# Attention scores of a tile in three rows, and up to two tiles between scores and the sum over values

## The chip, the cores and the metric

One core of a Trainium2 chip runs the whole program in one launch. The metric is the device time of that launch in microseconds (us), as the median of several runs. All data and all matmuls are float32.

## What is computed

The input `x` has 4 batches of 384 channels on a 32 x 32 grid (1024 positions). Two layers follow each other.

Layer 0 adds to `x` a two-dimensional selective scan of its group norm. Each batch is scanned in four directions; per direction and channel 16 states follow `h = h * exp(dt * A) + dt * u * B`, and the output is the sum of `h * C` over the states. The four directions are added, normalised over the channels and put through GELU.

Layer 1 treats the positions as tokens `t` of 384 numbers:

```python
t = t + attention(layernorm(t))    # 6 heads of 64; a token sees itself and the 64 before it
t = t + experts(layernorm(t))      # 4 experts 384 -> 1536 -> 384, the best 2 of each token, weighted
```

In the reference the attention of a head is `softmax(mask(q k^T / 8)) v`, and the heads' outputs are multiplied by a gate and a 384 x 384 matrix.

## The kernel before, in words

**Scan.** A batch makes 192 scan steps, 768 in all. A step covers 32 channels x 4 states of one direction over the 1024 positions, as a `[128, 1024]` tile: ScalarE makes the decay `exp(dt * a)` (`decay`, into one of two PSUM tiles `dA`), GpSimd multiplies by B (`times_b`), VectorE scans (`scan`), GpSimd or VectorE multiplies by C (`times_c`), and TensorE sums the states (`fold_y`, into a bank `ps_y`). `time_steps` prepares `dt`.

**Tokens.** When the scan of a batch is complete, `tokens(b)` (line 967) takes its 1024 tokens as 8 tiles of 128, `TILES = 3` of them in flight at once (line 1202). A tile goes through `tile(a)`: load (`yl`, `tt`), norm, GELU, norm, transposes, the queries `q` and keys `k`, the last 64 keys of the tile before (line 1048, after that tile is in `scored`), the values `v`. Then it waits at line 1065 until fewer than `CORES` tiles are in the list `core`. Inside the core it makes the scores (`score`, line 1071: for a pair of head pairs and one head of each pair, matmuls into a bank `ps_s`, then a masked copy with row maximum by VectorE), gives back `q` (line 1093), takes the exponentials on ScalarE in place (line 1099), turns them by transposes (`turn`, line 1106: one head pair into a bank `ps_p`, copied to `pt`, of which there are 3), takes a row for the result `o` (line 1125), sums over the values into a bank `ps_o`, scales (line 1143) and leaves the core (line 1148). The output matrix, a norm and the router's logits follow.

**Experts.** `route(n)` takes half a batch (4 tiles), ranks the experts of its tokens and scatters the tokens to slots in DRAM sorted by expert (`scatter`, row `tks`). A batch makes 19 expert tiles of 128 slots, 76 in all: `hidden` runs 72 matmuls into banks `ps_hid`, `output` 24 matmuls into a bank `y_ff`. `combine(b)` (line 1464) gathers each token's two results, adds them to the residual and writes the output; before the last batch it takes four rows at once (line 1474) for one tile.

**Shared stocks.** A `Stock` (line 78) is a set of buffers that a generator waits for. What matters here: `rows`, `NROW = 10` buffers of `[128, 384]`, shared by tokens (`yl`, `tt`, `xt`, `q`, `v`, `o`, `ot`, `xlt`), routing (`tks`) and combining (`cb`); `srows`, 4 buffers of `[128, 384]` for the scores of one tile; `pts_`, 3; `keys`, 2; `banks`, 4 PSUM banks for everything but `dA`. A waiter for one buffer is served in order of its rank (0 for the scan's banks, 1, and `HID_RANK = 2` for `ps_hid`); a waiter for several is served when so many are free. When the last scan is done, the scan's large buffers join `rows` and its two PSUM tiles join `banks` (lines 879 to 886).

**Order of the work.** Nothing is ordered by hand. While the program is built, `Machine` (line 218) runs all these generators against a model of the five engines with estimated durations, and emits each instruction when the model would start it. Among those that could start, the one with the lowest ready time plus bias goes first: `EARLY = -6` us for tokens and routing, 0 for the scan, `LATER = +6` us for the expert tiles and for combining. On the chip each engine then runs its queue in that fixed order. A change of a stock or of a limit can so move any later instruction of the program.

**Constants.** `b2_sb`, the experts' output bias, is a `[4, 384]` tile loaded at line 421 and used at line 1502 with the router's weights `gt` (line 1480). `gt_sb`, a `[32, 384]` tile of ones and zeros (lines 446 to 455), is used by the group norm.

Of the kernel before, what the change touches and what calls it, by code (L numbers as in the profile page):

```python
# [11 lines left out]
F32 = mybir.dt.float32  # L12
# [5 lines left out]
P = 128  # L18
B, D, HH, WW = 4, 384, 32, 32
L = HH * WW  # L20
T = D // P
# [4 lines left out]
GROUPS = 32  # L26
# [7 lines left out]
KW = WIN + P  # L34
NE, HID = 4, 4 * D
# [14 lines left out]
GELU_BIAS = EARLY  # L50
FAVOUR = 1.0
TILES, EPS, NZ = 3, 1e-5, 7
CORES = 1
NEG = -1.0e30


# [336 lines left out]
def conv_attn_hybrid(  # L393
# [7 lines left out]
    nc = tc.nc  # L401
    const = ctx.enter_context(tc.tile_pool(name="const", bufs=1))
    dram = ctx.enter_context(tc.tile_pool(name="dram", bufs=2, space=bass.MemoryType.DRAM))

    def const_load(src, shape, name):
        dst = const.tile(shape, F32, name=name)
        nc.sync.dma_start(dst, src)
        return dst
# [9 lines left out]
    vb_sb = const_load(vb.rearrange("(t p) -> p t", p=P), [P, T], "vb_sb")  # L418
    gw_sb = const_load(gw, [P, T, NE], "gw_sb")
    gb_sb = const_load(gb.partition_broadcast(P), [P, NE], "gb_sb")  # L420
    b2_sb = const_load(b2, [NE, D], "b2_sb")

    ident = const.tile([P, P], F32, name="ident")
    make_identity(nc, ident)
# [15 lines left out]
        base=0, channel_multiplier=1,  # L440
# [2 lines left out]
        gm, gm, pattern=[[-P, T], [GC, GROUPS]], compare_op=ALU.is_ge, fill=0.0,  # L443
        base=GC - 1, channel_multiplier=-1,
    )
    gt_sb = const.tile([GROUPS, D], F32, name="gt_sb")
    nc.gpsimd.memset(gt_sb, 1.0)
    nc.gpsimd.affine_select(
        gt_sb, gt_sb, pattern=[[1, D]], compare_op=ALU.is_ge, fill=0.0,
        base=0, channel_multiplier=-GC,  # L450
    )
    nc.gpsimd.affine_select(
        gt_sb, gt_sb, pattern=[[-1, D]], compare_op=ALU.is_ge, fill=0.0,
        base=GC - 1, channel_multiplier=GC,
    )

    mask = const.tile([P, KW], F32, name="mask")
# [3 lines left out]
        base=0, channel_multiplier=1,  # L461
# [3 lines left out]
        base=WIN, channel_multiplier=-1,  # L465
# [3 lines left out]
        base=0, channel_multiplier=-1,  # L469
# [7 lines left out]
        base=0, channel_multiplier=-1,  # L477
# [6 lines left out]
    m = Machine(nc)  # L484
# [7 lines left out]
    with tc.tile_pool(name="setup", bufs=1) as setup:  # L492
# [12 lines left out]
            base=0, channel_multiplier=1,  # L505
# [3 lines left out]
        for j in range(JB):  # L509
            ps = banks.now("ps_al")  # L510
# [17 lines left out]
    work = ctx.enter_context(tc.tile_pool(name="work", bufs=1))  # L528
# [5 lines left out]
    xbs, xbts, hss, ybs = (  # L534
        Stock(m, work, tag, n, [P, D]) for tag, n in (("xb", 1), ("xbt", 2), ("hs", NHS), ("yb", 1))
    )
    srows = Stock(m, work, "sr", 4 * CORES, [P, D])
    us_all = Stock(m, work, "u", 2, [P, L])
    eds = Stock(m, work, "ed", 3, [P, HB])
    keys = Stock(m, work, "key", 2, [P, T * KW])  # L540
# [40 lines left out]
    def copy(dst, src):  # L581

        if on_vector():
            yield from dve.tensor_copy(dst, src)
        else:
            yield from act.copy(dst, src)

    def on_vector():
        lead = FAVOUR if count_of["scan"] < NSLOT else 0.1
        return m.clock["dve"] + lead < m.clock["act"]  # L590
# [376 lines left out]
    def tokens(b):  # L967
# [18 lines left out]
        def tile(a):  # L986
# [11 lines left out]
            ps = yield from three("ps_y0", w)  # L998
            yield from normal_of(w, ps)
            g = yield from three("ps_g", w)  # L1000
            mm = Calls()
# [8 lines left out]
            ps = yield from three("ps_t", tt)  # L1010
            yield from normal_of(w, ps)
            xt = yield from rows.take("xt")
            ps = yield from three("ps_x1", w)
# [7 lines left out]
            for n, (w, dst) in enumerate(  # L1021
                ((wq, q[:, :D].rearrange("p (t l) -> p t l", t=T)), (wk, kv[:, :, :P]))
            ):
                ps = yield from banks.take("ps_qk")
                mm = Calls()
# [26 lines left out]
            ps = yield from banks.take("ps_v")  # L1052
            mm = Calls()
# [10 lines left out]
            n_keys = KW if a else P  # L1064
            yield lambda: len(core) < CORES
            core.append(a)
            mx = rp.tile([P, 2, HEADS], F32, tag="mx", name="mx")
            sums = rp.tile([P, HEADS], F32, tag="sums", name="sums")
            s = yield from srows.take("s", n=4)

            def score(hps, j):
                ps = yield from banks.take("ps_s")
                r = slice(j * HD, (j + 1) * HD)
                mm = Calls()
                for n, hp in enumerate(hps):
                    mm.matmul(
                        ps[:, n * KW : n * KW + n_keys],
                        q[r, ts(hp, P)], k[r, hp * KW : hp * KW + n_keys],
                        start=True, stop=True,
                    )  # L1080
                yield from pe.all(mm)
                for n, hp in enumerate(hps):
                    h = 2 * hp + j
                    c = slice(n * KW, n * KW + n_keys)
                    yield from dve.tensor_tensor_reduce(
                        s[hps[0] + j][:, c], ps[:, c], mask[:, :n_keys], 1.0, NEG,
                        ALU.add, ALU.max, mx[:, 0, h : h + 1],
                    )
                banks.give(ps)
# [5 lines left out]
            for hp in range(T):  # L1095
                for j in range(2):
                    h = 2 * hp + j
                    sj = s[hp // 2 * 2 + j][:, hp % 2 * KW : hp % 2 * KW + n_keys]
                    yield from act.activation(
                        sj, sj, AF.Exp, bias=mx[:, 1, h : h + 1], scale=scale,  # L1100
                        accum_out=sums[:, h : h + 1],
                    )
# [1 line left out]
            pts = {}  # L1104

            def turn(hp):
                base, c0 = hp // 2 * 2, (hp % 2) * KW
                pt = yield from pts_.take("pt")
                ps = yield from banks.take("ps_p")
                mm = Calls()  # L1110
                for j in range(2):
                    mm.transpose(ps[:, ts(j, P)], s[base + j][:, c0 : c0 + P], ident)
                for j in range(2 if a else 0):
                    mm.transpose(ps[:, ts(2 + j, P)], s[base + j][:, c0 + KW - P : c0 + KW], ident)
                yield from pe.all(mm)
                if hp > 0:
                    srows.give(s[base], s[base + 1])
                yield from copy(pt[:, : 2 * P], ps[:, : 2 * P])
                if a:
                    yield from copy(pt[WIN:, 2 * P :], ps[WIN:, 2 * P : 4 * P])  # L1120
                banks.give(ps)
                pts[hp] = pt
# [4 lines left out]
            mm = Calls()  # L1127
# [22 lines left out]
            ps = yield from three("ps_ot", o)  # L1150
# [3 lines left out]
            ps = yield from banks.take("ps_pr")  # L1154
            on_act = not on_vector()
            mm = Calls()
# [10 lines left out]
            for o in range(T):  # L1167
                c = ts(o, P)
# [12 lines left out]
            ps = yield from three("ps_t2", tt)  # L1181
# [6 lines left out]
            ps = yield from three("ps_xt", tt)  # L1188
            rows.give(tt)
            yield from copy(xt[:, :D], ps[:, :D])  # L1190
            mm = Calls()
# [272 lines left out]
    def combine(b):  # L1464

        def one(a):
            n, a_in = 2 * b + a // PT, a % PT
            if b == B - 1:
                yield lambda: n in routed
            xs, idx, p, eid, gate = routed[n]  # L1470
            if b == B - 1:
                o, gt = yield from rows.take("cb", n=2)
            else:
                o, gt, *gs = yield from rows.take("cb", n=4)
            yield from sp.dma_start(
                o[:, :D].rearrange("p (t l) -> p t l", t=T), t2dr[b][:, :, ts(a, P)]
            )
            ps = yield from banks.take("ps_gt")
            yield from pe.transpose(ps[:NE, :P], p[:, a_in, :], ident)
            yield from copy(gt[:NE, :P], ps[:NE, :P])  # L1480
            banks.give(ps)
            if b == B - 1:
                yield lambda: ("experts", b) in have
                gs = yield from rows.take("cb", n=2)
            for n in range(2):
                yield from pool.indirect_dma_start(
                    out=gs[n][:, :D], out_offset=None, in_=ysdr[b % 2],
                    in_offset=bass.IndirectOffsetOnAxis(ap=idx[:, n, a_in : a_in + 1], axis=0),
                )
            yield m.settled(*gs)  # L1490
            ps = yield from banks.take("ps_c")
            yield from act.activation(ps[:, :D], gs[0][:, :D], AF.Copy, scale=gate[:, 0, a_in : a_in + 1])
            yield from dve.scalar_tensor_tensor(
                gs[0][:, :D], gs[1][:, :D], gate[:, 1, a_in : a_in + 1], ps[:, :D], ALU.mult, ALU.add
            )
            mm = Calls()
            for t in range(T):
                c = ts(t, P)
                mm.matmul(ps[:, c], gs[0][:, c], ident, start=t == 0, stop=False)
            for t in range(T):  # L1500
                c = ts(t, P)
                mm.matmul(ps[:, c], b2_sb[:, c], gt[:NE, :P], start=False, stop=t == T - 1)
            yield from pe.all(mm)
            rows.give(gt, *gs)
            yield from dve.tensor_tensor(o[:, :D], ps[:, :D], o[:, :D], ALU.add)
            banks.give(ps)
            yield from sp.dma_start(
                out[b].rearrange("(t p) h w -> p t (h w)", p=P)[:, :, ts(a, P)],
                o[:, :D].rearrange("p (t l) -> p t l", t=T),
            )  # L1510
            rows.give(o)

        yield from m.together([one(a) for a in range(NT)], 2 if b < B - 1 else NT, LATER)
        have.add(("out", b))

# [82 lines left out]
```

## Time and profile before

| | |
|---|---|
| median of 3 runs | 3890.63 us (3870.85 to 3907.89) |
| the profiled execution | 3882.5 us, its span 3880.8 us |
| TensorE matmul, busy | 3033.4 us (78%), 15868 matmuls |
| VectorE, busy | 2940.7 us (76%) |
| GpSimd, busy | 2824.4 us (73%) |
| ScalarE, busy | 2226.8 us (57%) |
| mean granted TensorE clock | 0.822 of full speed |
| DMA | 953.65 MB, 246 GB/s |
| last scan step starts | 3201.9 us |

Read it as two stretches. Until 3202 us the scan runs, with the tokens and experts of finished batches beside it; after that there is no scan, and what is left are the remaining expert tiles, the tokens of the last batch and their experts. The shares in the table are averages over both.

The timeline gives the stages of the tokens, from the first transposes of the first tile to those before the last tile's logits: 782 to 1154 us for batch 0, 1617 to 2194 for batch 1, 2461 to 2904 for batch 2 and 3236 to 3499 for batch 3. Expert tiles leave (`yb`) from 1100 to 1613 us for batch 0, 2074 to 2868 for batch 1, 2907 to 3495 for batch 2 and 3510 to 3835 for batch 3.

### The profile page before, as it was taken

What the parts mean: (1) busy time and instruction counts of PE and PEld (TensorE: products, weight loads), DVE (VectorE), ACT (ScalarE), POOL (GpSimd) and SP (SyncE); (2) the same over time, 40 slices, a digit from 0 to 9 for tenths busy, and PEclk for the clock granted to TensorE, in tenths of its full rate; (3) what the DMA queues carried; (4) which work ended last, traced back from release to release, by engine and by line L of the source; (5) the groups of instructions that cost most, each with busy time, mean ns of one, the idle gap of its engine ahead of it and who ended that gap; (6) DMA issues with size and microseconds to landing.
All of it is one profiled execution on the core that took longest, in us unless ns stands there. A gap on an engine that the chain in (4) does not pass through costs nothing. (4 is left out here: it accounts for less than half of the span.)

```text
span 3880.8 us, 50273 instructions
## 1 busy us (share of the span) xinstructions
PE 3033.4 (78%) x15868; PEld 1841.7 (47%) x15868; DVE 2940.7 (76%) x3358; ACT 2226.8 (57%) x4017; POOL 2824.4 (73%) x1474
## 2 busy tenths in 40 slices
PE   2555555577697988777768889899787899998997
PEld 1100010045464555344345545566555557876886
DVE  2999999998888998888888899988788992332001
ACT  2545454467586777755557767778675763432221
POOL 1999989988898877888888699889787981012001
PEclk6555556678798999876678989899898999998997
DMA  5775775544478998734357989776568975459995
GB/s 202 266 273 204 270 268 203 174 143 149 171 253 333 341 374 324 285 127 164 112 208 254 329 301 347 270 254 213 203 228 295 388 272 184 136 167 327 318 318 182
DMA packets 394145, 953.65 MB, mean 246 GB/s; under 512 B 49620, under 2 KB 173400, under 8 KB 393880
## 3 DMA queue, kind: packets, MB, share of 16 engines
q1 hardware_dynamic: 385688, 925.27, 68.1%
q0 software_dynamic: 8192, 25.17, 1.9%
q8 instruction: 126, 2.06, 0.2%
q14 instruction: 139, 1.14, 0.1%
HBM read 786.39 MB, written 182.78 MB: 250 GB/s over the span
## 5 line engine op out<-in xcount | busy, mean ns | idle before, releaser
L148 POOL TENSOR_TENSOR z<-dts,bc 128x1024 f32<-128x1024 f32 x768 | 1792.9, 2359 | 186.7 <-PE ps_y L159 105.8
L148 ACT ACTIVATE dA<-dts,a 128x1024 f32<-128x1024 f32 x768 | 854.6, 1118 | 536.8 <-DVE z L148 512.1
L159 PE MATMUL ps_y<-z,fold 128*32 128x512 f32 x3072 | 725.8, 765 | 436.2 <-POOL z L148 237.2
L148 DVE TENSOR_TENSOR_SCAN dA<-dA,z 128x1024 f32<-128x1024 f32 x409 | 935.6, 2288 | 93.2 <-ACT dA L148 77.7
L148 POOL TENSOR_TENSOR z<-z,bc 128x1024 f32<-128x1024 f32 x359 | 841.7, 2355 | 110.8 <-DVE z L148 96.2
L148 DVE TENSOR_TENSOR_SCAN z<-dA,z 128x1024 f32<-128x1024 f32 x359 | 807.8, 2276 | 31.6 <-ACT dA L148 28.6
L159 PEld LDWEIGHTS ps_hid<-xbt,w_sb 128*128 128x128 f32 x5472 | 667.0, 198 | 137.2 <-issue 38.3
L159 PE MATMUL y_ff<-w_sb,hs 128*128 128x384 f32 x1824 | 680.8, 515 | 58.5 <-ACT hs L159 46.4
L159 PE MATMUL ps_hid<-xbt,w_sb 128*128 128x128 f32 x5472 | 692.0, 284 | 33.1 <-ACT hs L148 8.2
L148 DVE TENSOR_TENSOR z<-dA,bc 128x1024 f32<-128x1024 f32 x409 | 499.1, 1220 | 13.8 <-DVE dA L148 0.5
L159 PEld LDWEIGHTS ps_y<-z,fold 128*32 128x32 f32 x3072 | 93.1, 120 | 872.8 <-POOL z L148 412.8
L148 ACT ACTIVATE hs<-ps_hid,bb 128x128 f32<-128x128 f32 x912 | 274.1, 365 | 391.8 <-PE ps_hid L159 320.2
L159 PEld LDWEIGHTS y_ff<-w_sb,hs 128*128 128x128 f32 x1824 | 341.3, 199 | 314.9 <-issue 65.9
L148 POOL DMA_INDIRECT cb<-ysdr,idx x64 | 62.6, 979 | 293.7 <-DMA ysdr<-yb 269.8
L159 POOL TENSOR_TENSOR rn<-rn,half 128x1 f32<-128x1 f32 x96 | 52.7, 549 | 266.7 <-DVE rn L159 209.0
L148 DVE COPY yb<-y_ff 128x384 f32<-128x384 f32 x22 | 12.2, 556 | 251.5 <-PE y_ff L159 204.9
L148 POOL DMA_INDIRECT xsdr<-tks,idx x64 | 65.2, 1018 | 146.5 <-DVE idx L159 58.4
L148 ACT ACTIVATE ed<-ps_dt,dtb_sb 128x512 f32<-128x512 f32 x192 | 125.8, 681 | 67.6 <-PE ps_dt L148 59.8
L148 PE MATMUL ps_dt<-xd,dtw_sb 12*128 12x512 f32 x192 | 136.7, 822 | 24.7 <-DMA dtw_sb<-in_dtw_dram 14.2
L148 DVE TENSOR_TENSOR ps_dt<-ps_dt,ed 128x512 f32<-128x512 f32 x192 | 132.6, 690 | 12.3 <-ACT ps_dt L148 9.5
L148 ACT COPY ed<-ps_dt 128x512 f32<-128x512 f32 x96 | 56.0, 584 | 124.8 <-DVE ed L148 124.5
L304 ACT ACT_TABLE_LOAD x80 | 102.6, 1283 | 2.2 <-PEq L1583 0.8
(204 smaller groups left out, 3411.2 us busy)
## 6 DMA issues: line engine op xcount, KB each, us to landing
w_sb<-wl SPq DMA_DIRECT2D x608, 576.0 KB
dts<-dtr SPq DMA_DIRECT2D x384, 512.0 KB
bc<-xdr SPq DMA_DIRECT2D x128, 512.0 KB
dtr<-ed SPq DMA_DIRECT2D x192, 256.0 KB
ub<-udr SPq DMA_DIRECT2D x48, 512.0 KB
yp<-ydr SPq DMA_DIRECT2D x96, 256.0 KB
ydr<-yp SPq DMA_DIRECT2D x96, 256.0 KB
wl<-in_w_dram SPq DMA_DIRECT2D x32, 576.0 KB
```

The source lines that it names most:

```text
L148: return getattr(self.real, op)(*a, **k)
L159: getattr(self.real, op)(*a, **k)
L304: self.nc.scalar.add_instruction(mybir.InstLoadActFuncSet(name=self.nc.get_next_instruction_name(), act_func_set_id=EXP_LN_SET,))
```

## The change

- `CORES` goes from 1 to 2: two tiles may be between the start of their scores and the scaling of their result.
- The scores of a tile lie in three rows of `[128, 384]` in place of four: one row for each pair of heads, its two heads side by side. `srows` has 3 x 2 = 6 buffers in place of 4.
- `turn` gives a row back as soon as its own head pair is turned. Before, two rows held the heads of two pairs and were given back after the second of these.
- `b2_sb` and `gt_sb` become two parts of one tile of 36 partitions; the bias lies on partitions 32 to 35, and so the router's weights that are multiplied with it are copied to partitions 32 to 35 of `gt`.

```diff
-CORES = 1
+CORES = 2
...
-    b2_sb = const_load(b2, [NE, D], "b2_sb")
+    group_rows = const.tile([GROUPS + NE, D], F32, name="group_rows")
+    gt_sb, b2_sb = group_rows[:GROUPS], group_rows[GROUPS:]
+    nc.sync.dma_start(b2_sb, b2)
...
-    gt_sb = const.tile([GROUPS, D], F32, name="gt_sb")
...
-    srows = Stock(m, work, "sr", 4 * CORES, [P, D])
+    srows = Stock(m, work, "sr", T * CORES, [P, 2 * KW])
...
-            s = yield from srows.take("s", n=4)
+            s = yield from srows.take("s", n=T)
...
                     yield from dve.tensor_tensor_reduce(
-                        s[hps[0] + j][:, c], ps[:, c], mask[:, :n_keys], 1.0, NEG,
+                        s[hp][:, j * KW : j * KW + n_keys], ps[:, n * KW : n * KW + n_keys], mask[:, :n_keys], 1.0, NEG,
                         ALU.add, ALU.max, mx[:, 0, h : h + 1],
                     )
...
-                    sj = s[hp // 2 * 2 + j][:, hp % 2 * KW : hp % 2 * KW + n_keys]
+                    sj = s[hp][:, j * KW : j * KW + n_keys]
...
-                base, c0 = hp // 2 * 2, (hp % 2) * KW
...
-                    mm.transpose(ps[:, ts(j, P)], s[base + j][:, c0 : c0 + P], ident)
+                    mm.transpose(ps[:, ts(j, P)], s[hp][:, j * KW : j * KW + P], ident)
                 for j in range(2 if a else 0):
-                    mm.transpose(ps[:, ts(2 + j, P)], s[base + j][:, c0 + KW - P : c0 + KW], ident)
+                    mm.transpose(ps[:, ts(2 + j, P)], s[hp][:, (j + 1) * KW - P : (j + 1) * KW], ident)
                 yield from pe.all(mm)
-                if hp > 0:
-                    srows.give(s[base], s[base + 1])
+                srows.give(s[hp])
...
-            yield from copy(gt[:NE, :P], ps[:NE, :P])
+            yield from copy(gt[GROUPS : GROUPS + NE, :P], ps[:NE, :P])
...
-                mm.matmul(ps[:, c], b2_sb[:, c], gt[:NE, :P], start=False, stop=t == T - 1)
+                mm.matmul(ps[:, c], b2_sb[:, c], gt[GROUPS : GROUPS + NE, :P], start=False, stop=t == T - 1)
```

More of the change, by code (lines that the diff above doesn't have):

```diff
@@ L1083, in score @@
                     h = 2 * hp + j
-                    c = slice(n * KW, n * KW + n_keys)
                     yield from dve.tensor_tensor_reduce(
-                        s[hps[0] + j][:, c], ps[:, c], mask[:, :n_keys], 1.0, NEG,
+                        s[hp][:, j * KW : j * KW + n_keys], ps[:, n * KW : n * KW + n_keys], mask[:, :n_keys], 1.0, NEG,
                         ALU.add, ALU.max, mx[:, 0, h : h + 1],
```

## The prediction

> **What bounds the kernel now.** I read the page first, slice by slice.
>
> ```profile
> PE   2555555577697988777768889899787899998997
> ...
> DVE  2999999998888998888888899988788992332001
> ...
> POOL 1999989988898877888888699889787981012001
> PEclk6555556678798999876678989899898999998997
> ```
>
> A digit is a fortieth of the span, 97 us. Up to slice 33 VectorE and GpSimd are 70 to 90% and more busy: the scan sets the time. From slice 34 (3202 us) both fall and TensorE is at 90% or more: it sets the rest. So there are two prices: what lengthens or shortens the scan, and how much TensorE work is left when it ends. Next, the busy times by stage:
>
> ```profile
> core 0: us, PE busy (x) PEld busy (x) DVE busy (x) ACT busy (x) POOL busy (x), PEclk, DMA share, GB/s
> 194.00:776.00 582.00, 311.19 (x766) 44.96 (x768) 570.47 (x390) 279.68 (x321) 553.08 (x241) 0.58 0.67 232
> ...
> 1164.00:1600.00 436.00, 379.36 (x2048) 230.36 (x2047) 387.03 (x319) 308.80 (x513) 351.69 (x157) 0.93 0.94 349
> 1616.00:2194.00 578.00, 438.68 (x2163) 258.52 (x2159) 492.95 (x604) 363.74 (x656) 497.77 (x271) 0.74 0.55 185
> ...
> 3204.00:3840.00 636.00, 603.23 (x3801) 488.39 (x3801) 125.98 (x474) 204.77 (x594) 52.61 (x83) 0.97 0.72 240
> ```
>
> Scan alone: VectorE idle 2%. Scan and experts: 11%. Scan and the tokens of batch 1: 15%. After the scan TensorE is idle for 33 of 636 us. Third, how fast expert tiles run (24 `y_ff` matmuls each):
>
> ```profile
> 2074.00:2551.00 477.00, 122.59 (x312) 60.70 (x312) 0.00 (x0) 6.22 (x13) 0.91 0.83 297
> 2551.00:2868.00 317.00, 44.20 (x121) 22.48 (x120) 0.53 (x1) 2.07 (x5) 0.92 0.67 227
> 2868.00:3204.00 336.00, 100.55 (x264) 49.47 (x264) 0.00 (x0) 5.55 (x12) 0.92 0.85 307
> ```
>
> That is 13 tiles in 477 us (36.7 us each), 5 in 317 (63 each, beside the tokens of batch 2), 11 in 336 (30.5 each). From 2074 us expert work is always waiting, so an earlier start means more tiles done by 3202. Left after the scan:
>
> ```profile
> L159 PE MATMUL ps_hid<-xbt,w_sb 128*128 128x128 f32 x1872 | 232.0, 280 | 7.0 <-DMA w_sb<-wl 6.1 <-PE ps_hid L159 0.9
> L159 PE MATMUL y_ff<-w_sb,hs 128*128 128x384 f32 x648 | 229.2, 493 | 2.3 <-ACT hs L159 2.0 <-ACT hs L148 0.4
> ```
>
> 1872/72 = 26 and 648/24 = 27 tiles, at 232.0/26 + 229.2/27 = 17.4 us of TensorE each. This is the price of a tile left over.
>
> Last, where tokens wait for the core. In TensorE's timeline of batch 1, `ps_v` belongs to the third tile, `ps_p` and `ps_o` to the second:
>
> ```profile
> 1694.88 2.10 PE L159 MATMUL ps_v<-wv,xt 128*128 128x384 f32 x6
> ...
> 1705.58 1.12 PE L159 MATMUL ps_p<-ident,s 128*128 128x128 f32 x4 [0.55 <-ACT pt L148]
> ...
> 1745.10 1.62 PE L159 MATMUL ps_c<-ident,cb 128*128 128x128 f32 x6 [2.07 <-DVE cb L148]
> ...
> 1748.22 5.57 PE L159 MATMUL ps_o<-v,pt 128*128 128x64 f32 x24
> ...
> 1757.58 1.65 PE L159 MATMUL ps_s<-k,q 64*128 64x192 f32 x4
> ```
>
> The second tile has turned its scores at 1706 and sums only at 1748, right after `ps_c` of `combine(0)`, which took four rows at 1702.6 (its load `cb<-t2dr`) and gives three back there: what is late is the row for `o`. The third tile, ready at 1697, scores at 1757.6, after the second has left the core, and holds `q`, itself a row, all that time. Following each tile so, 12 of 32 start their scores 6.7 to 60.6 us after `ps_v`, where the others need 1.5 to 4. Less 2.5 us each that is 26, 64, 50 and 19 us of core wait in batches 0 to 3.
>
> **What the Trainium skill says.** "Perfetto Trace Analysis", Optimization Strategy: a gap that repeats on an engine that should be saturated can mean too few buffers for the next tile. The trace agrees: the 42 us between `ps_p` and `ps_o` is such a hole. "TensorE: Matmul & The Clock Gate", What picks the tile position: the row position follows the operands' start partition, 0, 32, 64 or 96, so the bias on partition 32 is a legal place. The same page, LDWEIGHTS: a weight load costs by columns, not by contraction rows. The trace agrees: 254 ns for the 4-row load beside 263 ns for the 128-row one of `ps_c`.
>
> **The change part by part.**
>
> *Three rows for four.* The masked copy stays 192 of 350 ns (last score shape 255), the exponentials 192 of about 440, the transposes 360 of 307: same counts and shapes, 0 us. A row that is free one transpose earlier only matters to another tile's scores, and that needs the second place in the core.
>
> *Bias on partitions 32 to 35.* 192 matmuls of 367 ns, 32 copies of 254 ns; no row shows them on another partition. 0 us taken; if each `ps_c` matmul grew by 60 ns, the last eight tiles (48 matmuls, which nothing covers) would add 3 us. `gt_sb` now shares a tile with a DMA issued at 6.05 us. If its `MEMSET` (1.06 us, GpSimd) waited for that landing, about 8.6 as for the next load, what is queued behind it would move by 7.6 us: mask, `before` and `sel_j`, for which the matmuls at 8.6 and so the first `xn` load at 13.1 wait. `sel_j` ends at 6.8, so 5.8 us would be exposed. I take 0, range 0 to 6.
>
> *Two tiles in the core.* No instruction is added; the order changes. The third tile's scores go ahead of the second's sum. Queued behind these 12 matmuls (4.5 us by the rows of 373 ns) and 6 copies (2.1 us on VectorE) are a scan step and a sum of states; they run once either way. Next late: the transposes of the second occupant, since 3 `pt` serve one tile, then the row for `o`.
>
> 1. Core wait removed, over three tiles in flight: 26/3 = 9 us of stage for batch 0, 50/3 = 17 for batch 2, 19/3 = 6 for the last.
> 2. Batch 1: `q` comes back about 55 us sooner in that hole and can serve as `o` or as the next tile's `yl`. Bounds for its first four tiles, which open its experts: 0 (combining holds its rows for about 58 us a tile whatever happens) to 100 (this 52 us hole and the third tile's next one, 1781 to 1822, both go). I take 40.
> 3. Experts of batch 1 start 40 + 9 = 49 us earlier: 49/36.7 = 1.3 tiles. Batch 2's stage 17 us shorter, at 30.5 in place of 63 us a tile: 0.3. Together 1.6 tiles x 17.4 = 28 us less after the scan.
> 4. These 1.6 tiles now run beside the scan. Pace there: 3.44 us a step alone, 4.00 with 15 tiles in 436 us (109 steps): 61/15 = 4 us a tile; from 3007 to 3201 it is 3.46, so nearly 0. I take 2.5: +4 us.
> 5. Stages shorter by 9 + 40 + 17 = 66 us, where VectorE idles some 16% in place of 9%: -5 us.
> 6. Last batch 6 us sooner; TensorE's 33 idle us can pay for it: -6 us.
>
> Sum: -28 + 4 - 5 - 6 = -35 us. Against the profiled 3882.5 (span 3880.8 and 1.7 around it) this gives 3847 us. The median shown, 3890.6, lies 8 above the profiled execution and the runs spread over 37, so against the median it is -1.1%.
>
> **Rivals.**
>
> *The wait only moves (no change).* With 3 `pt` and no free row, the second occupant scores and then stands before `turn` or `o`. For it: combining takes four rows again at 1773 and 1846. Against it: `q` is a row, and in batches 0 and 2, which hardly combine, rows are free. 3868 to 3898, middle 3883.
>
> *More than forecast.* Both holes of batch 1 go: 109/36.7 + 0.5 = 3.5 tiles x 17.4 = 61, and idle time as far as 5 and 6 allow, some 20: 3790 to 3825, middle 3805.
>
> *Slower: experts lose their PSUM banks.* Four banks serve everything; one tile scoring holds up to two `ps_s`, two tiles four, and `ps_hid` has the last rank. Place: 2551 to 2868 us, where experts already fall to 63 us a tile. If that became 120, 2.4 of 5 tiles would be left over, 41 us, and in the other stages as much again: up to 3965. It decides from about 2 tiles more than 27 after 3202 us. Against it: scores last 5 to 10 us of a tile's 100. But a new order of the whole program can cost the same anywhere, so I give it weight.
>
> **Numbers.** Forecast (3825 to 3868) 0.40, more 0.17, no change 0.15, slower (3895 to 3970) 0.28. Faster by over 1% (below 3851.7; 1% is about what a measurement here can tell from no change) holds five eighths of the forecast and all of "more": 0.42. Slower by over 1% (above 3929.5): 0.20 of the 0.28. Within: 0.38. The range 3790 to 3945 leaves out the lower edge of "more" and the worst third of "slower", under 0.2 together; the forecast's own is 3825 to 3868.
>
> **What would show it.** Right: scores within 4 us of `ps_v` on nearly all tiles; tokens of batch 1 complete before 2150 us; its first expert tile leaves before 2040; 25 or 26 tiles of `y_ff` after the last scan; last scan within 10 us of 3202. Wrong: scores early but `ps_p` or `ps_o` no earlier (no change); 29 tiles or more left, or the last scan beyond 3230 (slower).

## The result, and the profile after

The changed kernel takes 3875.03 us (median of 13 runs, 3860.63 to 3881.28) beside 3888.22 for the kernel before (13 runs): ratio 0.9963, 95% interval [0.9946, 0.9980]. It is 13 us faster, 0.4%, where 1.1% was forecast. The profiled execution took 3876.8 us with a span of 3875.1.

The slices of the page after the change, again 97 us each:

```profile
PE   2555555578888899778696898878688799998997
...
DVE  2999999998888889888889898898878893332001
...
POOL 1999989999879878889897777989788991012001
PEclk8555556687888999768698999887789899998997
```

From slice 9 on TensorE shows 7 8 8 8 8 where it showed 7 7 6 9 7: the tokens of batch 0 take 314 us in place of 373 and its experts start sooner. From slice 25 on it shows 8 8 7 8 6 8 where it showed 9 8 9 9 7 8: lower from about 2330 to 2910 us. The last eight slices are as before. The windows of three stretches tell more: the token stage of batch 1, a stretch named below, and the time from the last scan step to the last expert tile.

```profile
core 0: us, PE busy (x) PEld busy (x) DVE busy (x) ACT busy (x) POOL busy (x), PEclk, DMA share, GB/s
1589.00:2051.00 462.00, 370.25 (x2007) 239.48 (x2006) 393.08 (x525) 308.73 (x596) 406.57 (x230) 0.78 0.56 191
...
2562.00:2879.00 317.00, 232.56 (x1203) 144.25 (x1201) 266.56 (x361) 202.91 (x382) 271.12 (x154) 0.75 0.52 175
...
3209.00:3830.00 621.00, 595.07 (x3792) 484.57 (x3790) 124.78 (x465) 202.82 (x601) 53.63 (x82) 0.97 0.73 244
```

The token stage of batch 1 took 462 us in place of 578. The same three questions as before: how fast do expert tiles run,

```profile
core 0: us, PE busy (x) PEld busy (x) DVE busy (x) ACT busy (x), PEclk, DMA share, GB/s
1959.00:2562.00 603.00, 168.00 (x432) 83.93 (x432) 0.00 (x0) 8.36 (x18) 0.92 0.83 301
2562.00:2879.00 317.00, 10.06 (x24) 4.78 (x24) 0.00 (x0) 0.49 (x1) 0.75 0.52 175
2879.00:3209.00 330.00, 95.16 (x252) 47.58 (x252) 0.00 (x0) 5.22 (x11) 0.93 0.83 295
```

(the `y_ff` matmuls alone, 24 for a tile), what is left after the scan,

```profile
L159 PE MATMUL ps_hid<-xbt,w_sb 128*128 128x128 f32 x1854 | 226.8, 278 | 0.6 <-ACT xbt L148 0.6
L159 PE MATMUL y_ff<-w_sb,hs 128*128 128x384 f32 x639 | 225.1, 491 | 2.7 <-DMA w_sb<-wl 1.6 <-ACT hs L159 1.1
```

and where tokens wait. The middle row of the first is the finding: in the 317 us from 2562 to 2879 one expert tile ran. Before, 5 ran from 2551 to 2868. The experts of batch 1 were finished 306 us sooner (2562 for 2868), and then there was nothing to do. Left after the scan are 1854/72 = 25.8 and 639/24 = 26.6 tiles, where 26 and 27 were left before.

In TensorE's timeline of batch 1 the first `ps_v` and `ps_s` are the third tile's, the `ps_p` and `ps_o` of 1663.73 and 1666.43 are the second's, and the last `ps_p` and `ps_o` are the third's again:

```profile
1654.82 2.15 PE L159 MATMUL ps_v<-wv,xt 128*128 128x384 f32 x6
...
1658.38 0.93 PE L159 MATMUL ps_s<-k,q 64*128 64x192 f32 x8
...
1663.73 0.66 PE L159 MATMUL ps_p<-ident,s 128*128 128x128 f32 x4 [0.68 <-ACT pt L148]
...
1666.43 3.03 PE L159 MATMUL ps_o<-v,pt 128*128 128x64 f32 x24
...
1675.48 0.66 PE L159 MATMUL ps_p<-ident,s 128*128 128x128 f32 x4
...
1705.65 1.62 PE L159 MATMUL ps_c<-ident,cb 128*128 128x128 f32 x6 [4.33 <-DVE cb L148]
...
1712.11 5.57 PE L159 MATMUL ps_o<-v,pt 128*128 128x64 f32 x24
```

The third tile's scores start 3.6 us after its values instead of 63, and the second's sum starts 2 us after the end of its transposes instead of 42. But the third tile is turned at 1676 and sums only at 1712, right after `ps_c` of `combine(0)`: it waits 36 us, as it did before. Not every hole of batch 1 is closed. And in batch 2, the third tile:

```profile
2577.10 1.30 PE L159 MATMUL ps_p<-ident,s 128*128 128x128 f32 x8 [0.31 <-ACT pt L148]
...
2617.30 1.62 PE L159 MATMUL ps_c<-ident,cb 128*128 128x128 f32 x6 [9.15 <-DVE cb L148]
...
2621.77 5.41 PE L159 MATMUL ps_o<-v,pt 128*128 128x64 f32 x24
```

This is the hole that batch 1 had before: from the end of the transposes the sum waits 43 us for its row, until `combine(1)`, which loaded at 2566.6, gives rows back after `ps_c`. `combine(1)` gathered from 2887 to 3096 us before, beside no tokens. Since the experts of batch 1 end sooner it now gathers from 2590 to 3034, on top of the tokens of batch 2. Their stage grew from 444 to 494 us (2469 to 2963), and its first four tiles, which open the first experts of batch 2, ended at 2742 instead of 2710. They open only 5 of its 19 expert tiles (`SIZES`, lines 42 and 43, is 5 and 14); the other 14 wait for all eight tiles of the tokens, which are complete at 2965 instead of 2908.

### The profile page after: what moved, and what is told of

It is laid out like the page before. It is cut to its first block, busy times and chain, and to the rows that moved or that the text cites. A ratio compares the mean times of both kernels' runs of the same rounds, so it can differ in the third digit from the quotient of the medians.

```text
span 3875.1 us, 50356 instructions
## 1 busy us (share of the span) xinstructions
PE 3042.1 (79%) x15892; PEld 1859.1 (48%) x15892; DVE 2953.5 (76%) x3353; ACT 2231.7 (58%) x4034; POOL 2805.7 (72%) x1465
## 5 line engine op out<-in xcount | busy, mean ns | idle before, releaser
L148 DVE TENSOR_TENSOR_SCAN dA<-dA,z 128x1024 f32<-128x1024 f32 x418 | 956.0, 2287 | 81.4 <-ACT dA L148 68.0
L148 POOL TENSOR_TENSOR z<-z,bc 128x1024 f32<-128x1024 f32 x350 | 822.3, 2359 | 133.1 <-DVE z L148 125.6
L148 DVE TENSOR_TENSOR_SCAN z<-dA,z 128x1024 f32<-128x1024 f32 x350 | 788.4, 2276 | 43.1 <-ACT dA L148 37.4
L148 DVE TENSOR_TENSOR z<-dA,bc 128x1024 f32<-128x1024 f32 x418 | 509.8, 1220 | 14.7 <-DVE dA L148 0.9
```

Source lines behind the costliest of these rows:

```text
L148: return getattr(self.real, op)(*a, **k)
```

## The experiments

All edits are to the changed kernel unless said otherwise, and ratios are to the kernel before, run on the same chip. The theory "supply" says: the experts of batch 1 start sooner and end sooner, but those of batch 2 open only when its own tokens have come through, so the earlier start buys nothing. Rivals: "banks" (two scoring tiles take PSUM banks from others) and "order" (a new order of the whole program, by chance).

**The layout alone.** `CORES = 1`, all else as changed.

> The changed kernel with one place in the core (three score rows, the bias beside the group matrix). Theory 'supply': the layout does nothing by itself, 3880 to 3896 us, and the token stages are as long as in the kernel before (batch 1 some 578 us). Rival 'order' (the 13 us are a chance of a new order of the program): any value from 3865 to 3910, since this kernel's order is new too. Rival 'banks' (two scoring tiles take PSUM banks from the expert tiles): as before, 3880 to 3896.

Measured: 3890.81 us, ratio 0.9999 [0.9983, 1.0016], the token stage of batch 1 from 1617 to 2194 us, as before. Three rows, the earlier giving back and the bias on other partitions are worth nothing together that can be measured. This also shows how far one execution can be read: its last scan step starts at 3196 us, that of the kernel before at 3202, with the same token times.

**The combining held back.**

```diff
             yield lambda: ("experts", b) in have or (b == B - 1 and 2 * b + 1 in routed)
+            yield lambda: b == B - 1 or all(("token", b + 1, a) in have for a in range(NT))
```

> The changed kernel, but combine(b) of the first three batches waits until the tokens of batch b + 1 are complete, so that it takes no rows during that token stage. Theory 'supply' (the expert tiles of batch 1 end at 2562 us and those of batch 2 can only start at 2879, because combine(1) has moved onto the tokens of batch 2 and holds four of the ten rows): the first four tiles of batch 2 end about 80 to 100 us sooner, 3 to 5 more expert tiles are done when the scan ends, 3800 to 3840 us. Rival 'banks': the token stage of batch 2 is no shorter without the combining, 3865 to 3885. Rival 'order': no direction, 3855 to 3895.

Measured: 3814.56 us, ratio 0.9804 [0.9779, 0.9829]; the best of all. The first four tiles of batch 2 end at 2654 us, 88 sooner than with the change alone, its first expert tile leaves at 2771 instead of 2879, and 23.8 `y_ff` tiles are left instead of 26.6 after the scan, whose last step starts at 3190. That is 2.8 tiles, a little under the 3 to 5 expected. The token stage of batch 2 takes 373 us instead of 494, with the same two places and the same four banks, which "banks" had denied. The expert tiles in three stretches:

```profile
1916.00:2528.00 612.00, 167.30 (x432) 81.61 (x432) 0.00 (x0) 8.76 (x19) 0.91 0.87 311
2528.00:2771.00 243.00, 8.71 (x24) 4.24 (x24) 0.00 (x0) 0.43 (x2) 0.82 0.49 163
2771.00:3190.00 419.00, 123.96 (x318) 60.89 (x318) 0.00 (x0) 6.58 (x14) 0.91 0.85 307
```

The dry stretch, in which almost no expert tile runs, is still 243 us, but it ends 108 us sooner.

**Two places in some batches only.** Line 1066 of the changed kernel (1065 before) with `len(core) < (CORES if b == B - 1 else 1)`, and with `b < B - 1`.

> Two places in the core for the tokens of the last batch alone, one for the other three. Theory 'supply': the whole gain of the change comes from the tokens after the scan, so 3870 to 3882 us. Rival 'order' and rival 'banks': the gain belongs to no stage, 3880 to 3896.

> Two places in the core for the tokens of the first three batches, one for the last. Theory 'supply': the stages of batches 0 and 1 are shorter by 60 and 140 us as in the changed kernel, but as many expert tiles are left after the scan as before (27), so 3880 to 3895 us. Rival 'order': any value from 3865 to 3910. If the earlier experts had been worth what was forecast, it would be 3850 to 3865.

Measured: 3886.04 us, ratio 0.9996 [0.9981, 1.0010], for the last batch alone; 3871.81, 0.9949 [0.9929, 0.9968], for the first three. That the whole gain comes from the last batch was wrong: a second place there is worth nothing that can be measured (TensorE was already busy for 249 of the 263 us of that stage in the kernel before), and two places in the first three batches alone bring as much as the change. With two places there the token stages are those of the changed kernel (batch 1 from 1591 to 2052), and still the gain is 0.5%, not what the earlier experts had been forecast to bring. The time lies between the two ranges that had been named, 3850 to 3865 and 3880 to 3895.

**One combine held.** The hold above for `b == 1` alone, and for `b == 0` alone.

> The changed kernel, and only combine(1) waits, until the tokens of batch 2 are complete; combine(0) runs beside the tokens of batch 1 as in the changed kernel. Theory 'supply': what the change lacks is work for the experts between 2562 and 2879 us, so this hold alone brings nearly all of the 60 us that holding all three brought: 3815 to 3835 us, the first expert tile of batch 2 leaves before 2790, at most 24.5 tiles are left after the scan. Rival (the earlier experts of batch 1 made the gain of the other run): 3855 to 3875.

> The changed kernel, and only combine(0) waits, until the tokens of batch 1 are complete. Theory 'supply': the experts of batch 1 start and end some 40 us sooner still, and that buys nothing, because those of batch 2 start as late as in the changed kernel: 3862 to 3882 us, some 26.5 tiles left after the scan. Rival (earlier experts of batch 1 make the gain): 3820 to 3845.

Measured: 3853.67 us, 0.9910 [0.9885, 0.9935], with `combine(1)` held; 3891.47, 1.0006 [0.9994, 1.0018], with `combine(0)` held. Neither fell in its range, but the order of the two is the one that "supply" asked for. Holding `combine(0)` brought the experts of batch 1 forward again (1913 to 2530 us), and that not only bought nothing: 28.3 tiles were left, and the 0.4% that the change had gained was gone. Holding `combine(1)` took the first four tiles of batch 2 from 2742 to 2684 us and left 23.0 tiles; of the gain some went back, in this execution, through a scan that ended at 3222 us and 46 us of idle TensorE after it (25 before that edit).

The traces show what each hold does to the wait in question. For every tile, take the time from the end of its last `ps_p` to the start of its first `ps_o`, and add up the eight tiles of a batch. The other columns follow batch 2: when the last of its tokens has its logits, when its sixth expert tile leaves (the first of those that wait for all eight token tiles), how long it is from there to the last scan step, and how many tiles are left then:

| kernel | waits, batch 1, us | waits, batch 2, us | tokens complete | sixth tile | to last scan step, us | tiles left |
|---|---|---|---|---|---|---|
| before | 196 | 34 | 2908 | 3064 | 138 | 27.0 |
| the change | 107 | 128 | 2965 | 3070 | 139 | 26.6 |
| only `combine(0)` held | 29 | 98 | 2976 | 3091 | 96 | 28.3 |
| only `combine(1)` held | 108 | 24 | 2868 | 2976 | 246 | 23.0 |
| all three combines held | 29 | 35 | 2819 | 2955 | 235 | 23.8 |

Each of the single holds takes most of the wait out of the batch whose tokens it protects, and not out of the other. What is left after the scan goes with the sixth tile, that is, with the end of the tokens of batch 2, and not with the start of the experts of batch 1.

**The hold without the second place.** The kernel before, with the hold for the first three batches.

> The kernel before (one place in the core, its own layout) with combine(b) held until the tokens of batch b + 1 are complete. Theory 'supply': the first four tiles of batch 2 end near 2710 us as before, since no combining ran beside them there either; the experts of batch 1 end sooner, and those of batch 2 follow from about 2830: 3835 to 3865 us. The difference to the held kernel with two places (3815) is then what the second place is worth once the rows are free. If the second place is worth nothing, 3815; if the hold helps only two places, 3880 to 3895.

Measured: 3821.46 us, 0.9833 [0.9809, 0.9856]. Better than expected: the experts of batch 1 end at 2549 us, the first four tiles of batch 2 at 2654, not 2710. The likely reason is that in the kernel before the experts of batch 1 still ran beside them; this was not tested apart. Whether the second place adds anything to the hold is not settled: 0.9804 and 0.9833 have overlapping intervals.

**Rows in place of the second place.** `CORES = 1` and `NROW = 13`.

> The changed kernel with one place in the core, and the three score rows that are saved added to the ten shared rows. Theory 'rows' (in batch 1 the second place helps because it gives q, a shared row, back sooner): three more rows shorten the stage of batch 1 from 578 us to 400 to 500 as the second place does; no experts of batch 2 sooner than the first four tiles of batch 2 at 2710, so 3865 to 3890 us. If it is the core's order and not the rows, the stage of batch 1 stays above 550 us and the time at 3880 to 3896.

Measured: 3892.21 us, 1.0011 [0.9999, 1.0024]. The stage of batch 1 falls to 436 us (1620 to 2056), below the changed kernel's 462, and its sums wait 28 us in all, where the same kernel with ten rows had 197: rows are what it lacked. And again it buys nothing (the time is 2 us above the range of "rows"): the experts of batch 1 end at 2595 us, `combine(1)` gathers from 2608 on, the sums of batch 2 wait 134 us, its first four tiles end at 2734 and its sixth expert tile leaves at 3071, as with the change (3070). Here only one tile scores at a time, so that this loss can't be put down to two scoring tiles and their banks.

**The early start taken back.** The tokens stay early, only the routing waits.

```diff
             yield lambda: all(("token", b, a0 + a) in have for a in range(PT))
+            yield lambda: n != 2 or count_of["scan"] >= 477
```

> The changed kernel, but the routing of the first half of batch 1 waits for the 477th scan step, near 1980 us: the experts of batch 1 start about as late as in the kernel before (first leaving tile near 2080 in place of 1959), though the tokens stay early. If an earlier start of the experts is worth what the forecast said (36.7 us for a tile of 17.4), this costs 120/36.7 x 17.4 = 57 us: 3920 to 3940. Theory 'supply': the early start only makes the experts run out earlier, so it costs nothing: 3860 to 3885 us, and the experts of batch 1 still end before those of batch 2 start.

Measured: 3851.30 us, 0.9913 [0.9887, 0.9938]. Starting the experts of batch 1 143 us later (first tile out at 2102 us for 1959) did not cost 57 us; it is faster than the change. Its expert tiles:

```profile
2102.00:2756.00 654.00, 167.58 (x432) 82.58 (x432) 0.55 (x1) 7.75 (x17) 0.92 0.79 285
2756.00:2815.00 59.00, 9.76 (x25) 4.90 (x24) 0.00 (x0) 0.50 (x1) 0.86 0.72 254
2815.00:3191.00 376.00, 110.04 (x276) 54.53 (x277) 0.00 (x0) 5.71 (x12) 0.91 0.85 303
```

The dry stretch shrinks to 59 us, `combine(1)` starts at 2782 in place of 2590, the first four tiles of batch 2 end at 2683 in place of 2742, and the experts of batch 2 come 64 us sooner, the sixth tile 57 us sooner (3013). So this edit does two things: it takes the early start back and it keeps `combine(1)` off most of the tokens of batch 2. It shows that the early start was worth less than what it set off, not that an early start is worth nothing; the held kernel, where the experts of batch 1 start early (1916 us) and `combine(1)` is out of the way, is faster still. The 3851 us lie below the range of "supply" too.

**Banks.** In line 1091, `score` one at a time in place of two.

> The changed kernel, but a tile makes its scores one bank at a time in place of two, so that two tiles hold at most two of the four banks. Rival 'banks' (two scoring tiles keep the experts and the scan from their banks, which ate the gain): 3840 to 3865 us. Theory 'supply': 3865 to 3885, no direction.

Measured: 3890.59 us, 1.0013 [1.0001, 1.0025]. Fewer banks for the scores are no gain but undo the change's: the stage of batch 1 is back at 577 us. "Banks" had asked for 3840 to 3865. The test is not a clean one, since it also lengthens the scores of a tile (in batch 1 from 7.4 to 10.9 us on average); the hold, which works without touching the banks, and the thirteen-row kernel say more against "banks". The range of "supply" was missed too.

**More rows, or more tiles, with the hold.** One place, 13 rows and the hold; then the hold, two places and `TILES = 4`.

> One place in the core, thirteen shared rows, and all three combines held. Theory 'rows': with the combining out of the way the ten rows are enough for three tiles, so three more bring nothing over the held kernel with one place (3821): 3812 to 3830 us. If rows are still short then: below 3805.

> The held kernel with two places, and four tiles of a batch in flight in place of three. If the first four tiles of batch 2 are what the experts wait for, and rows suffice, they end 20 to 50 us sooner: 3790 to 3812 us. If four tiles run out of rows (up to four a tile) or share engines that are already full: 3812 to 3840.

Measured: 3832.83 us, 0.9869 [0.9844, 0.9893], and 4747.69 us, 1.2230 [1.2199, 1.2262]. The first is 3 us above its range: without combining beside the tokens, three more rows bring nothing. Four tiles were far worse than either expectation:

```profile
PE   3555555554545554555555488989999999999998
...
DVE  3999999999999999999999953433232120110100
```

The tokens of batch 0 start at 781 us and the last of them is through at 2911, after the scan (2744): no token instruction runs from 841 to 2751. By then each of the four tiles holds `tt` and `xt` and two hold `q`, which makes ten rows; the first waits for its `v`, and no other can give a row back. Nothing moved until the end of the scan added its buffers to the stock. The scan ran almost alone, its last step starting at 2744 us, and the rest took another 2000 us.

## Why the prediction was right in direction and wrong in size

*Bounds and prices.* The two stretches and the price of a tile hold: 226.8/25.8 + 225.1/26.6 = 17.3 us of TensorE for a tile after the scan (17.4 forecast).

*The hole of 42 us.* It was read as a gap on an engine that should be saturated. It is a gap in one tile's own chain: from 1685 to 1754 us VectorE was busy for 61 of 69 us and TensorE for 48. That it comes from too few buffers holds, as the thirteen rows show.

*The layout at 0 us.* Right: ratio 0.9999 with one place. The `ps_c` matmul with the bias has a median of 416 ns on partitions 32 to 35 as it had on 0 to 3; the `MEMSET` still starts at 1.06 us and the first `xn` load at 13.1.

*Step 1, core wait.* Right in kind: on all 32 tiles the scores start at most 6.4 us after the end of `ps_v`, on 28 within 4. Too small for batch 0, whose stage fell by 59 us (373 to 314), not 9; wrong in sign for batch 2.

*Step 2, batch 1.* Right in place, and under-sized: the first four tiles ended 98 us sooner (1836 for 1934), not 40. That is close to the upper bound of 100, but not for its reason: of the two holes that it named, the third tile's, 36 us, is still there. The thirteen-row kernel shows that rows were what was short; that it is the row of `q` in particular was not tested.

*Step 3, the step that failed.* It priced the earlier start of batch 1's experts at one tile for each 36.7 us, because "from 2074 us expert work is always waiting". That held for the kernel before, whose experts of batch 1 ended at 2868 us and those of batch 2 came out from 2907. With 115 us of earlier start (49 forecast) the price gives 115/36.7 = 3.1 tiles; 0.4 fewer `y_ff` tiles were left. For in the changed kernel work was not always waiting: the experts of batch 1 ended 306 us sooner, and then one tile ran in 317 us. In both kernels they are done long before the scan ends, so what is left after it depends on batch 2. Its first five expert tiles leave from 2879 us on in place of 2907, but then none leaves from 3017 to 3070, since the tokens of batch 2 are complete 57 us later, and the sixth comes 6 us later than before. From there to the last scan step it is 139 us, before 138: of the lead nothing remains. So the term that mattered was the stage of batch 2, priced at 0.3 tiles for 17 us less, and it became 50 us longer, because `combine(1)` follows the end of the experts of batch 1. I had read in batch 1 what combining does to tokens, and didn't ask where `combine(1)` would go once it was released sooner.

*Steps 4 and 5, the scan.* The last step starts at 3209 us for 3202, forecast 3201. Two executions with the same token times differ by 6, so this is not resolved.

*Step 6, last batch.* Not seen. TensorE's idle time from the last scan step to the last expert tile is 26 us for 30, and a second place there alone measures 0.9996, with an interval that is too wide to rule out 6 us.

*The signs.* Four of the five named for "right" came: early scores, the tokens of batch 1 by 2051 us, its first expert tile at 1959, the last scan step within 10 us of 3202. The fifth, 25 or 26 tiles left, carries the gain, and it did not come.

*The rivals.* "The wait only moves" gave the nearest time, 3883, and part of its mechanism is there: in batch 1 three of eight tiles still stand before `o` for 24 to 36 us, but the waits there fell from 196 to 107 us in all. The larger part it did not name: the wait that rose in batch 2, from 34 to 128. "Banks" as a loss is refuted, since the kernel did not get slower; as what ate the gain, nothing supports it, and the thirteen-row kernel loses the gain without it. "More than forecast" had the earlier start right, nearly 100 us, and failed on the same premise. That the direction came out right is partly luck: of the 28 us that were to come from tiles left over, some 7 came (0.4 x 17.3).

*What stays open.* Of the 13 us the two profiled executions show 6: 12 us less after the scan (a few tenths of a tile and some idle time) and 7 more before it. Where the rest lies was not found, only that two places in the first three batches are enough for it. "Order" is not excluded for these 13 us: five other kernels, each with an order of its own, measure 0.9996 to 1.0013, which speaks against it, but the two kernels that gain 0.4 and 0.5% share nearly the same order. For the hold it is an unlikely rival: all four kernels in which `combine(1)` is held, and three tiles are in flight, gain 0.9 to 2.0%, and the one in which only `combine(0)` is held gains nothing. Nor is it settled why the last scan step starts anywhere from 3184 to 3222 us in the kernels with three tiles in flight.

## What to carry to other kernels

An earlier start of a stage that feeds a bound is worth something only as far as its next supply is there: follow the backlog to its end, and look at what opens the stage after it, all of it and not only its first part. Ask of every stage that ends sooner what it releases, and which buffers that takes; here the released work took four of ten shared buffers from the tokens that the next supply depended on, and one line that holds it back is worth 1.7 to 2.0%, with the second place or without. A task that holds some buffers of a shared stock while it waits for more can stop everything: with four tiles in flight the tokens waited 1910 us for the stock to grow.

## What was not expected of the hardware

Nothing in the runs pointed to the hardware itself; every surprise was in the order of the work and its buffers. The two tile positions of the bias are alike (416 ns each), and the scan, run almost alone, starts its last step at 2744 us, where beside tokens and experts it does so at 3209.
